# A mixture-of-experts block with adapters: the shared first product by seven half-products over pairs of token groups, staged between the adapter products, and the table entries of all experts fetched together

## The chip, the cores and the metric

One Trainium2 chip, one core of it. The metric is the device time of one execution in microseconds (us), median of three runs. Engines: PE (TensorE, matmuls and weight loads), DVE (VectorE), ACT (ScalarE), POOL (GpSimd) and SP (SyncE, which here only issues transfers). Each engine works through its own instructions in order.

## What is computed

The input is x, 8 batches of 256 tokens, hidden size 1024, in fp32. Every batch has an adapter, chosen by a number in 3 to 7.

```
y      = einsum('bsi,boi->bso', x, weight[adapter_ids])
shared = (silu(g) * u) @ shared_w_down.T,   [g, u] = y @ shared_w_gate_up.T      (1024 -> 2 x 1024 -> 1024)
probs  = softmax(y @ gate_w.T);  the top 2 of 16 experts, their weights made to sum to 1
expert e: (silu(g) * u) @ w_down[e].T,      [g, u] = y @ w_gate_up[e].T          (1024 -> 2 x 256 -> 1024)
out    = x + shared + sum over a token's two experts of weight * expert(y)
```

## The kernel before

**Precision.** A product of fp32 values is made of three matmuls (`mm3`, L73): each operand is split into a high part (a copy rounded to fp32r, on ACT, L59) and a low part (the difference, on DVE, L60); high x high, high x low and low x high are summed in PSUM. `load_w` (L64) brings a weight tile of 128 x 1024 over SP's queue into one of four staging buffers (`st`) and splits it into one of seven buffers of `whl` (`hl`); so PE can have up to seven split tiles ahead of it.

**Tiling.** The 2048 tokens are four groups of 512, each of four blocks of 128 (16 blocks in all).
- `cond(b)` (L145) makes y for the 256 tokens of a batch: 96 matmuls of 512 columns; ACT copies PSUM to `yrow` and puts it in DRAM as `y_d`.
- `group_yt(g)` (L469) reads a group's y back, on POOL's queue (`yr`, L474), transposes it on DVE (L139) and splits it into `yt`.
- `route(g)` (L171): gate logits (16 matmuls of 512 columns, L175), softmax and top 2 on DVE (L194 to L225), each token's rank in its expert by small matmuls (L227 to L237), and eight scatters on POOL (L268), which put the token numbers into a table by expert, `tab_d`. The scatters write one table and go one after the other. The place in the table of a rank below 256 is interleaved (L254 to L260, 264), so that 32 rows with eight entries each can be read as runs.
- `shared_up(g)` (L284): 16 weight tiles of `sgu` x 24 matmuls of 512 columns (`sps`), SwiGLU on ACT and DVE (L278), the result split into `ht`. Four groups: 1536 matmuls.
- `shared_down(g)` (L307): 192 matmuls (`dps`) of a group; DVE adds them to `acc` (L325), which goes to DRAM.
- `experts` (L457): the experts in the order of their token counts, with a fixed capacity of 256 to 304 tokens each. `expert_rows` (L431) reads the entries of one expert (`ib`), POOL makes them places (`ix`, L428) and gathers rows of y in pieces of 256 columns (`yg`, L351); DVE transposes; 96 matmuls of 256 to 304 columns a half (`eps`); the down product (`ops`) goes to `os_d`.
- `combine` (L328): two gathers of rows of `os_d` for a block (L331, POOL), each multiplied and added on DVE (L337).

**Order.** The calls at the end of the function (L478 to L576) give the order; a scheduler then sets the order of each engine's instructions within it, from a model of their times. The order is: the first two adapter products, group 0, cond(2), route(0), half of shared_up(0), cond(3), the other half, group 1, cond(4), route(1), half of shared_down(0), and so on to route(3); shared_up(3), entries and rows of experts 0 and 1, shared_down(3); the 16 experts; shared_up(1) with the combine of eight blocks between its tiles, shared_down(1), shared_up(2) with eight more, shared_down(2). The rows of `combine` and the y blocks share four buffers (`yg`).

## Time and profile before

| | before |
|---|---|
| median of three runs | 1067.23 us (1064.14 to 1073.18) |
| profiled execution: span from first to last instruction | 1060.8 us |
| mean granted TensorE clock | 0.992 of full speed |
| PE busy | 1029.5 us (97%), 5181 matmuls |
| DVE, ACT, POOL busy | 657.7, 466.4, 292.1 us |
| moved by DMA | 243.86 MB, 230 GB/s on the mean |

The page of the profile gives for the profiled execution its span alone; no time of that execution around the span is recorded, so the span stands beside the median.

In the profile a group is a line of the kernel with an engine, an operation and a tile shape; "out<-in" are tile names; after the bar come busy time, mean ns of one, and the idle time of the engine before them with what ended it. In the forty slices a digit is the busy share in tenths, PEclk the granted clock in tenths. A row of the table by stretches gives the length, and for PE, PEld, DVE, ACT and POOL the busy us and the count, then PE's granted clock, the share of DMA time and GB/s. A row of waits gives us in total, times, and the longest. A landing time runs from a transfer's issue to its end. A row of the timeline gives start, length, and in brackets the idle time before it.

### The profile page before, as it was taken

What the parts mean: (1) busy time and instruction counts of PE and PEld (TensorE: products, weight loads), DVE (VectorE), ACT (ScalarE), POOL (GpSimd) and SP (SyncE); (2) the same over time, 40 slices, a digit from 0 to 9 for tenths busy, and PEclk for the clock granted to TensorE, in tenths of its full rate; (3) what the DMA queues carried; (4) which work ended last, traced back from release to release, by engine and by line L of the source; (5) the groups of instructions that cost most, each with busy time, mean ns of one, the idle gap of its engine ahead of it and who ended that gap; (6) DMA issues with size and microseconds to landing.
All of it is one profiled execution on the core that took longest, in us unless ns stands there. A gap on an engine that the chain in (4) does not pass through costs nothing.

```text
span 1060.8 us, 14494 instructions
## 1 busy us (share of the span) xinstructions
PE 1029.5 (97%) x5181; PEld 875.8 (83%) x5181; DVE 657.7 (62%) x918; ACT 466.4 (44%) x626; POOL 292.1 (28%) x332
## 2 busy tenths in 40 slices
PE   6989999999899899999999999999999999999997
PEld 5877888888677688889999999989988888888886
DVE  5676543765567745546877878777784768537321
ACT  5564342544344423314667666566473233122200
POOL 1000210001200223644666656545203423002000
PEclk9999999999899999999999999999999999999999
DMA  7986384567677443655788888787979987827201
GB/s 257 345 301 219 105 253 140 204 232 215 223 249 253 135 159 88 220 189 186 237 283 275 291 271 282 249 273 251 340 262 358 408 344 264 318 92 258 80 33 50
DMA packets 82557, 243.86 MB, mean 230 GB/s; under 512 B 14204, under 2 KB 23164, under 8 KB 82476
## 3 DMA queue, kind: packets, MB, share of 16 engines
q1 hardware_dynamic: 56060, 186.46, 52.6%
q0 software_dynamic: 15856, 47.87, 13.0%
q10 hardware_dynamic: 10560, 8.52, 2.4%
q8 instruction: 42, 0.69, 0.2%
q14 instruction: 39, 0.32, 0.1%
HBM read 203.11 MB, written 39.69 MB: 229 GB/s over the span
## 4 chain that ended last, share of the span: by engine, by line
PE 57%; DMA 5%; issue 5%; POOL 3%; DVE 3%; ACT 1%; POOLq 0%; DVEq 0%; ACTq 0%
PE sps L76 8%; PE sps L75 8%; PE sps L74 8%; PE dps L76 4%; PE dps L75 4%; PE dps L74 4%; PE eps L76 4%; PE eps L74 4%; PE eps L75 4%; POOL yg L351 3%; PE ops L76 2%; PE ops L75 1%; DMA y_d<-yrow 1%; PE ops L74 1%; PE ops L419 1%
## 5 line engine op out<-in xcount | busy, mean ns | idle before, releaser
L60 DVE TENSOR_TENSOR hl<-st,hl 128x1024 fp32r<-128x1024 f32 (+1 forms) x274 | 330.1, 1209 | 180.0 <-ACT hl L59 178.9
L59 ACT CAST hl<-st 128x1024 fp32r<-128x1024 f32 (+1 forms) x274 | 283.5, 1043 | 254.8 <-PE sps L76 79.0
L76 PE MATMUL sps<-yt,hl 128*128 128x512 f32 x512 | 199.5, 390 | 0.0
L75 PE MATMUL sps<-yt,hl 128*128 128x512 f32 x512 | 199.4, 389 | 0.0
L74 PE MATMUL sps<-yt,hl 128*128 128x512 f32 x512 | 198.9, 390 | 0.0
L351 POOL DMA_INDIRECT yg<-y_d,ix x128 | 149.9, 1171 | 40.1 <-issue 35.1
L74 PE MATMUL eps<-yte,hl 128*128 128x256 f32 (+6 forms) x512 | 147.6, 289 | 0.1
L76 PE MATMUL eps<-yte,hl 128*128 128x256 f32 (+6 forms) x512 | 147.5, 288 | 0.0
L75 PE MATMUL eps<-yte,hl 128*128 128x256 f32 (+6 forms) x512 | 147.0, 287 | 0.0
L76 PEld LDWEIGHTS sps<-yt,hl 128*128 128x128 f32 x512 | 96.1, 188 | 20.0
L74 PEld LDWEIGHTS sps<-yt,hl 128*128 128x128 f32 x512 | 96.2, 188 | 19.9
L75 PEld LDWEIGHTS sps<-yt,hl 128*128 128x128 f32 x512 | 96.1, 188 | 19.9
L74 PE MATMUL cps<-hl 128*128 128x512 f32 x256 | 100.8, 398 | 7.6 <-ACT hl L59 7.6
L75 PE MATMUL cps<-hl 128*128 128x512 f32 x256 | 102.2, 399 | 3.2 <-DVE hl L60 3.2
L76 PE MATMUL cps<-hl 128*128 128x512 f32 x256 | 101.7, 397 | 0.0
L76 PE MATMUL dps<-hl,ht 128*128 128x512 f32 x256 | 99.8, 390 | 0.0
L75 PE MATMUL dps<-hl,ht 128*128 128x512 f32 x256 | 99.6, 389 | 0.0
L74 PE MATMUL dps<-hl,ht 128*128 128x512 f32 x256 | 99.6, 389 | 0.0
L74 PEld LDWEIGHTS eps<-yte,hl 128*128 128x128 f32 x512 | 96.4, 188 | 1.1 <-DVE s L378 0.5
L75 PEld LDWEIGHTS eps<-yte,hl 128*128 128x128 f32 x512 | 96.5, 188 | 0.7
L76 PEld LDWEIGHTS eps<-yte,hl 128*128 128x128 f32 x512 | 96.3, 188 | 0.0
L474 POOL DMA_DIRECT2D yr<-y_d x24 | 13.4, 559 | 239.9 <-DMA y_d<-yrow 189.7
(153 smaller groups left out, 1307.5 us busy)
## 6 DMA issues: line engine op xcount, KB each, us to landing
st<-sgu SPq DMA_DIRECT2D x64, 512.0 KB, 3.7
st<-wgu SPq DMA_DIRECT2D x64, 512.0 KB, 3.8
st<-wc SPq DMA_DIRECT2D x63, 512.0 KB, 4.7
st<-sd SPq DMA_DIRECT2D x32, 512.0 KB, 3.9
st<-wd SPq DMA_DIRECT2D x32, 512.0 KB, 5.2
os_d<-o SPq DMA_DIRECT2D x32, 512.0 KB, 5.7
yr<-y_d POOLq DMA_DIRECT2D x24, 512.0 KB, 6.3
y_d<-yrow ACTq DMA_DIRECT2D x16, 512.0 KB, 8.9
```

The source lines that it names most:

```text
L59: nc.scalar.copy(hi, src)
L60: nc.vector.tensor_tensor(lo, src, hi.bitcast(F32), op=ALU.subtract)
L74: nc.tensor.matmul(ps, lhs[0], rhs[0], start=first, stop=False)
L75: nc.tensor.matmul(ps, lhs[0], rhs[1], start=False, stop=False)
L76: nc.tensor.matmul(ps, lhs[1], rhs[0], start=False, stop=last)
L351: nc.gpsimd.indirect_dma_start(out=r[:, t * 256 : (t + 1) * 256], out_offset=None, in_=y_d.rearrange("k a p f -> (k a p) f"), in_offset=ba ...
L419: nc.tensor.matmul(ps, a3[:, fi, :], w[fi][:, l, hs], start=(fi == 0 and l == 0), stop=(fi == 1 and l == 1))
L474: nc.gpsimd.dma_start(r, y_d[g * NB + k].rearrange("a (i t) f -> (a i) (t f)", t=4))
```

## The change

**Seven half-products.** For a pair of groups the product y x sgu is written as a 2 x 2 product: y is halved in the hidden dimension (b1., b2.) and in the pair's groups (b.1, b.2), the weights into four quarters (gate and up by the two halves). Seven products of halves, on sums of halves, take the place of eight: 4 x 24 x 7 = 672 matmuls of 512 columns a pair, before 768. They come in stages: a (two products), b (two), c (one) and d (two), four steps u each. Partial results are kept in fp32 in SBUF (`X`, `S`, `G`); stages b and c begin by copying `X` into PSUM on ACT (`seeded`). Sums of the y halves are made on DVE (`sums`). Sums of the weights are made on DVE for the first pair, stored in DRAM (`ss_d`, ACT's queue) and loaded as weights for the second. The operand halves are split into a ring of four buffers.

**Staging.** For the pair of groups 0 and 1 the stages stand between the adapter products cond(3) to cond(7) and the routes; for the pair of groups 2 and 3 they come after the experts, with the combine of the blocks between the steps. Shared_down(0) and (1) now stand between route(3) and the experts, (2) and (3) at the end.

**Routing.** Groups 1 to 3 are routed from blocks of 128 columns (64 matmuls of 128 columns in place of 16 of 512). The inputs are permuted ahead of the launch so that a table place is the rank itself.

**Entries.** The entries of experts 0 and 1 are read after route(3), those of the other 14 together after the rows of expert 1, with one set of `ix` for all.

**Buffers.** `whl` has five buffers, seven among the experts; PSUM is seven banks in a fixed turn; `combine` has two buffers for its rows (`cr`) and two for its sums (`ca`); pools are opened and closed by phase.

```diff
-    whl = ctx.enter_context(tc.tile_pool(name="whl", bufs=7))
-    big = ctx.enter_context(tc.tile_pool(name="big", bufs=2))
-    rows = ctx.enter_context(tc.tile_pool(name="rows", bufs=3))
+    whl = ctx.enter_context(tc.tile_pool(name="whl", bufs=5))
+    ttp = ctx.enter_context(tc.tile_pool(name="ttp", bufs=2))
...
+    banks = [pacc.tile([P, 512], F32, tag=f"acc{k}", name=f"acc{k}") for k in range(7)]
+    turn = [0]
+    def bank():
+        turn[0] += 1
+        return banks[turn[0] % 7]
...
+    def transpose_to(dst, r, nt):
         nc.vector.transpose(
-            tv.rearrange(order, t=nt),
+            dst.rearrange("p b (t i) -> p t b i", t=nt),
             r[:, : nt * 256].rearrange("p (t b j) -> p t b j", t=nt, b=NC),
         )
+    def transposed(r, nt):
+        tt = ttp.tile([P, 1024], F32, tag="tt", name="tt")
+        tv = tt[:, : NC * 32 * nt].rearrange("p (b n) -> p b n", b=NC)
+        transpose_to(tv, r, nt)
+        return tv
...
+    def route(g, parts):
         lp = psm.tile([P, GT], F32, tag="sm", name="lp")
-        for c in range(NC):
-            for l in range(2):
-                nc.tensor.matmul(lp, gpk[:, c * 2 * E : c * 2 * E + P], yt[:, l, c, :], start=(c == 0 and l == 0), stop=(c == NC - 1 and l == 1))
+        n0 = 0
+        for get, n in parts:
+            for c in range(NC):
+                for l in range(2):
+                    nc.tensor.matmul(
+                        lp[:, n0 : n0 + n],
+                        gpk[:, c * 2 * E : c * 2 * E + P],
+                        get(c)[l],
+                        start=(c == 0 and l == 0),
+                        stop=(c == NC - 1 and l == 1),
+                    )
+            n0 += n
...
-            # place of rank 32t + i: 8i + t below MAIN, the rank itself from MAIN on
-            v.tensor_scalar(ov, rank, float(MAIN), None, op0=ALU.is_lt)
-            v.tensor_scalar(tq, rank, -15.5, 1.0 / 32, op0=ALU.add, op1=ALU.mult)
-            v.tensor_copy(sli, tq)
-            v.tensor_copy(tq, sli)
-            v.tensor_scalar(u, rank, 7.0, None, op0=ALU.mult)
-            v.scalar_tensor_tensor(u, tq, -255.0, u, op0=ALU.mult, op1=ALU.add)
-            v.tensor_tensor(u, u, ov, op=ALU.mult)
...
-            v.tensor_tensor(sl, sl, u, op=ALU.add)
...
-    def shared_up(yt, ht, fs=range(SI // P), also=None):
-        for f in fs:
-            pp = []
-            for j in range(2):
-                w = load_w(sgu[j * (SI // P) + f])
-                ps = pacc.tile([P, GT], F32, tag="acc", name="sps")
-                for c in range(NC):
...
+    def y_block(tb, ys):
+        r = ys.tile([P, 1024], F32, tag="yr", name="yr")
+        nc.gpsimd.dma_start(r, y_d[tb].rearrange("a (i t) f -> (a i) (t f)", t=4))
+        return r
...
+    def operand(ring, src):
+        t = []
+        for k in range(2):
+            op = ring.tile([P, 2, 2, 512], FR, tag="op", name="op")
+            split(op[:, 0], op[:, 1], src[:, 2 * k : 2 * k + 2, :])
+            t.append(op)
+        return t
...
+    def blocks_of(srcs):
+        for src in srcs:
+            t = whl.tile([P, 2, NC, P], FR, tag="whl", name="rb")
+            split(t[:, 0], t[:, 1], src)
+            yield (lambda c, t=t: [t[:, l, c, :] for l in range(2)]), P
...
+    class Up:
+        def __init__(self, first, raw, X, S, G, ring, ys, g0):
+            self.first, self.raw, self.X, self.S, self.G, self.ring, self.ys, self.g0 = first, raw, X, S, G, ring, ys, g0
+        def rows(self, n):
+            for k in range(NB):
+                r = y_block((self.g0 + n) * NB + k, self.ys)
+                transpose_to(self.raw[n][:, :, k * P : (k + 1) * P], r, 4)
+        def half(self, k, n):
+            return self.raw[n][:, 4 * k : 4 * k + 4, :]
+        def begin(self):
+            self.b11 = operand(self.ring, self.half(0, 0))
+            self.b21 = operand(self.ring, self.half(1, 0))
+        def sums(self):
+            v = nc.vector.tensor_tensor
+            t2 = self.S
+            for k in range(2):
+                q = slice(2 * k, 2 * k + 2)
+                b11, b12, b21, b22 = (self.half(r, n)[:, q, :] for r, n in ((0, 0), (0, 1), (1, 0), (1, 1)))
+                t = t2[:, q, :]
+                v(b12, b12, b11, op=ALU.subtract)
+                v(t, b22, b12, op=ALU.subtract)
+                v(b21, b21, t, op=ALU.subtract)
+                v(b11, t, b11, op=ALU.subtract)
+            self.t2 = operand(self.ring, t2[:, 0:4, :])
+            self.t3 = operand(self.ring, self.half(0, 0))
+            pair = lambda a: [a[:, 2 * k : 2 * k + 2, :].rearrange("p a n -> p (a n)") for k in range(2)]
+            at = pair(self.half(0, 0))
+            self.spare_b = [at, pair(self.S[:, 4:8, :]), at, at]
+            self.spare_d = [at, pair(self.half(1, 0))] * 2
+        def product(self, ps, w, m, ops, first):
+            for c in range(4):
+                lhs = [w[:, l, (4 * m + c) * P : (4 * m + c + 1) * P] for l in range(2)]
+                rhs = chunk(ops, c)
+                for i, (x, y) in enumerate(((0, 0), (0, 1), (1, 0))):
+                    nc.tensor.matmul(ps, lhs[x], rhs[y], start=(first and c == 0 and i == 0), stop=(c == 3 and i == 2), skip_group_check=True)
...
+        def made(self, i, u, st):
+            hl = whl.tile([P, 2, 1024], FR, tag="whl", name="shl")
+            split(hl[:, 0, :], hl[:, 1, :], st)
+            nc.scalar.dma_start(ss_d[i, u], st)
+            return hl
+        def sums_b(self, u):
+            if not self.first:
+                return load_w(ss_d[1, u]), load_w(ss_d[2, u])
+            v = nc.vector.tensor_tensor
+            a11, a21 = self.spare_b[u]
+            nc.gpsimd.dma_start(a11, sgu[0, 0, u])
+            nc.gpsimd.dma_start(a21, sgu[1, 0, u])
+            a22 = wst.tile([P, 1024], F32, tag="wst", name="a22")
+            nc.sync.dma_start(a22, sgu[1, 1, u])
+            v(a11, a11, a21, op=ALU.subtract)
+            v(a21, a21, a22, op=ALU.add)
+            v(a22, a22, a11, op=ALU.subtract)
+            w = self.made(1, u, a22), self.made(2, u, a11)
+            nc.scalar.dma_start(ss_d[0, u], a21)
+            return w
+        def sums_d(self, u):
+            if not self.first:
+                return load_w(ss_d[0, u]), load_w(ss_d[3, u])
+            s2, a12 = self.spare_d[u]
+            nc.gpsimd.dma_start(s2, ss_d[1, u])
+            nc.gpsimd.dma_start(a12, sgu[0, 1, u])
+            nc.vector.tensor_tensor(a12, a12, s2, op=ALU.subtract)
+            return load_w(ss_d[0, u]), self.made(3, u, a12)
+        def stage_a(self, u):
+            w1, w2 = load_w(sgu[0, 0, u]), load_w(sgu[0, 1, u])
+            ps = [bank() for m in range(2)]
+            for m in range(2):
+                self.product(ps[m], w1, m, self.b11, True)
+                nc.scalar.copy(self.X[:, 2 * u + m, :], ps[m])
+            for m in range(2):
+                self.product(ps[m], w2, m, self.b21, False)
+                nc.scalar.activation(self.G[:, 2 * u + m, :], ps[m], AF.Silu)
+        def seeded(self, u):
+            ps = [bank() for m in range(2)]
+            for m in range(2):
+                nc.scalar.copy(ps[m], self.X[:, 2 * u + m, :])
+            return ps
+        def stage_b(self, u):
+            w1, w2 = self.sums_b(u)
+            ps = self.seeded(u)
+            for m in range(2):
+                self.product(ps[m], w1, m, self.t2, False)
+                nc.scalar.copy(self.S[:, 2 * u + m, :], ps[m])
+            for m in range(2):
+                self.product(ps[m], w2, m, self.t3, False)
+                nc.scalar.copy(self.X[:, 2 * u + m, :], ps[m])
+        def stage_c(self, u):
+            if u == 0:
+                self.t4 = operand(self.ring, self.half(1, 0))
+            w = load_w(sgu[1, 1, u])
+            ps = self.seeded(u)
+            for m in range(2):
+                f = 2 * u + m
+                self.product(ps[m], w, m, self.t4, False)
+                nc.vector.tensor_tensor(self.G[:, f, :], self.G[:, f, :], ps[m], op=ALU.mult)
+        def stage_d(self, u):
+            if u == 0:
+                self.t1 = operand(self.ring, self.half(0, 1))
+                self.b22 = operand(self.ring, self.half(1, 1))
+            w1, w2 = self.sums_d(u)
+            ps = [bank() for m in range(2)]
+            for m in range(2):
+                f = 2 * u + m
+                self.product(ps[m], w1, m, self.t1, True)
+                nc.vector.tensor_tensor(self.X[:, f, :], ps[m], self.X[:, f, :], op=ALU.add)
+            for m in range(2):
+                f = 2 * u + m
+                self.product(ps[m], w2, m, self.b22, False)
+                nc.vector.tensor_tensor(self.S[:, f, :], ps[m], self.S[:, f, :], op=ALU.add)
+                nc.scalar.activation(self.S[:, f, :], self.S[:, f, :], AF.Silu)
+                nc.vector.tensor_tensor(self.S[:, f, :], self.S[:, f, :], self.X[:, f, :], op=ALU.mult)
...
+    def combine(rows, tb, base, dst):
+        ts = slice(tb * P, (tb + 1) * P)
+        a = rows.tile([P, 1024], F32, tag="ca", name="ca", bufs=2)
+        nc.sync.dma_start(a, base[ts, :])
+        for si, cw in ((s1i, c1), (s2i, c2)):
+            r = rows.tile([P, 1024], F32, tag="cr", name="cr", bufs=2)
+            nc.gpsimd.indirect_dma_start(
+                out=r,
+                out_offset=None,
+                in_=os_d[:, :],
+                in_offset=bass.IndirectOffsetOnAxis(ap=si[:, tb : tb + 1], axis=0),
+            )
+            nc.vector.scalar_tensor_tensor(a, r, cw[:, tb : tb + 1], a, op0=ALU.mult, op1=ALU.add)
+        nc.sync.dma_start(dst[ts, :], a)
...
+    def entries(ns):
+        for n in ns:
+            e = expert_id(n)
+            w = -(-CAPS[n] // 32)
+            nc.sync.dma_start(ib[:, n, :w], tab_d[ds(e * SLOTS, 32 * w), :].rearrange("(t i) o -> i (t o)", i=32))
+        segments(ix[:, ns[0] : ns[-1] + 1, :], ib[:, ns[0] : ns[-1] + 1, :])
...
+    up = Up(True, raw, X, S_, G, ring, ys, 0)
+    up.rows(0)
+    cond(2, ys)
+    up.begin()
+    route(0, [(lambda c: chunk(up.b11 if c < 4 else up.b21, c % 4), GT)])
+    cond(3, ys)
+    up.stage_a(0)
+    up.rows(1)
+    up.stage_a(1)
+    route(1, blocks_of([raw[1][:, :, k * P : (k + 1) * P] for k in range(NB)]))
+    up.stage_a(2)
+    up.stage_a(3)
+    cond(4, ys)
+    up.sums()
+    up.stage_b(0)
+    up.stage_b(1)
+    cond(5, ys)
+    up.stage_b(2)
+    up.stage_b(3)
+    cond(6, ys)
+    route(2, blocks_of(transposed(y_block(2 * NB + k, ys), 4) for k in range(NB)))
+    up.stage_c(0)
+    up.stage_c(1)
+    cond(7, ys)
+    up.stage_c(2)
+    up.stage_c(3)
+    for u in range(4):
+        up.stage_d(u)
+    route(3, blocks_of(transposed(y_block(3 * NB + k, ys), 4) for k in range(NB)))
+    close(px, pr)
...
+    entries([0, 1])
+    e0 = expert_rows(pa[1], 0)
+    shared_down(0, G, ring, ys, x, xs_d)
+    yt = expert_yt(pa[1], e0)
+    rs = expert_rows(pa[1], 1)
+    entries(range(2, E))
+    shared_down(1, S_, ring, ys, x, xs_d)
...
+    def some(k):
+        for tb in left[:k]:
+            combine(ys, tb, x if tb >= 2 * NB else xs_d, xs_d if tb >= 2 * NB else out)
+        del left[:k]
+    for u in range(4):
+        up.stage_a(u)
+        some(1)
+    up.sums()
+    for u in range(4):
+        up.stage_b(u)
+        some(1)
+    for u in range(4):
+        up.stage_c(u)
+        some(u % 2)
+    for u in range(4):
+        up.stage_d(u)
+        some(1)
+    close(px)
+    pc = pool("pc", 4)
+    shared_down(2, G, ring, pc[1], xs_d, out, ["acc"] * NB)
+    some(2)
+    shared_down(3, S_, ring, pc[1], xs_d, out, ["acc"] * NB)
```

## The prediction

> **What bounds the kernel now.** I read the busy row and the forty slices first, then the table by stretches, then the timeline of PE around one gap, then what DVE and POOL wait for, the groups, and the landing times.
>
> ```profile
> span 1060.8 us, 14494 instructions
> ...
> PE 1029.5 (97%) x5181; PEld 875.8 (83%) x5181; DVE 657.7 (62%) x918; ACT 466.4 (44%) x626; POOL 292.1 (28%) x332
> ...
> PE   6989999999899899999999999999999999999997
> ...
> PEclk9999999999899999999999999999999999999999
> ```
>
> PE is the bound: 31.3 us of the span are idle, in slices 1 to 3, 11, 14 and 40.
>
> ```profile
> 106.00:160.00 54.00, 54.00 (x244) 44.55 (x243) 26.44 (x51) 21.89 (x26) 10.77 (x9) 1.00 0.59 181
> ...
> 266.00:320.00 54.00, 48.41 (x193) 38.31 (x192) 33.13 (x35) 21.81 (x26) 8.54 (x8) 0.91 0.71 235
> 320.00:373.00 53.00, 47.06 (x205) 37.45 (x204) 37.89 (x108) 20.52 (x23) 9.18 (x9) 0.97 0.61 197
> ```
> ```profile
> 266.33 0.39 PE L74 MATMUL cps<-hl 128*128 128x512 f32 x1
> 269.37 0.79 PE L75 MATMUL cps<-hl 128*128 128x512 f32 x1 [2.65 <-DVE hl L60]
> 269.96 0.63 PE L76 MATMUL cps<-hl 128*128 128x512 f32 x1
> 270.39 0.63 PE L74 MATMUL cps<-hl 128*128 128x512 f32 x1
> ```
>
> The matmuls overlap, so the 390 ns of a group is not their price; the spacing of starts is: 45 of 512 columns between 14.78 and 25.00 us, 0.227 each. After a gap of 2.65 us they start 0.43 apart (269.96, 270.39): the granted clock is half. Four such spells cost 2.45, 2.05, 1.5 and 1.65 us, 7.6 in all. Work at full pace is thus 1060.8 - 31.3 - 7.6 = 1021.9; the start (7.6 until the first weights are split, 0.5, 2.5 of half clock) and the tail (6.7) are 17.3; the stalls between, clock included, 21.6.
>
> ```profile
> DVE tt L139 <- DMA yg<-y_d,ix: 31.3, 5, 14.0
> ...
> DVE sli L256 <- DMA tab_d<-tid,sli: 22.5, 3, 10.2
> ```
> ```profile
> r<-os_d,s1i POOLq DMA_INDIRECT x16, 7.7
> r<-os_d,s2i POOLq DMA_INDIRECT x16, 7.9
> ```
> ```profile
> yr<-y_d POOLq DMA_DIRECT2D x24, 512.0 KB, 6.3
> y_d<-yrow ACTq DMA_DIRECT2D x16, 512.0 KB, 8.9
> ```
>
> DVE is only 62% busy but works in order, and already waits 14.0 us at a stretch for gathers, 10.2 for scatters. PE hardly felt the first: seven split weight tiles lay ahead of it.
>
> **Part by part: what PE loses and gains.** The first product falls from 1536 to 1344 matmuls of 512 columns: 192 x 0.227 = -43.6 us. Routing of groups 1 to 3 trades 48 of 512 columns for 192 of 128: -10.9, and by the nearest row (280 columns start 0.127 apart, 512 0.227, so about 0.43 ns a column plus little) 0.061 each at the least, 0.127 at the most: +11.7 to +24.4; I take 0.075, near the slope, +14.4. Sum: 1021.9 - 43.6 - 10.9 + 14.4 = 981.8; with start and tail unchanged, 999.1 without a stall in between.
>
> **Engines that get more.** DVE: per pair 8 sums of 1024 columns, 14 operand splits, in the first pair 16 weight sums; at 1.23 us (row of L60: 1.21) 46.7 us a first pair, less 16 transposes of 2.00 that become 1.24 and 8 that go. ACT: 32 seeds and 32 drains of PSUM at 0.6, about 38. Neither reaches 80%; as busy time they cost nothing while PE has 980. The transfers grow by the 16 stores of sums on ACT's queue and 24 loads on POOL's, 512 KB each, and by 8 MB of combine's own tiles; the stretch from 800 to 853 us moved 390 GB/s with PE busy 53.0 of 53.0, so 230 on the mean leaves room. ACT issues those stores between its copies; I count nothing for it, since the copies of the next weights are some tiles ahead, and a store that waits for its sum would show as PE waiting on ACT's hl. POOL's loads are item 3. What counts is order, with five weight tiles ahead (27 us at 24 matmuls each) instead of seven (38), two more only among the experts.
>
> **New stalls, by place.** Each is the time until the last thing that PE needs, less PE's work ahead of it.
> 1. First route: the existing 3.4 us stays.
> 2. Stage a, u = 2, after cond(3). Its y is written and read back: 8.9 + 6.3, and issues, 17 us. Behind that wait stand on DVE two transposes, two splits of routing blocks, the eight sums, then the split of a weight: 13 x 1.23 = 16. Ready after 33 us; PE has 96 x 0.227 + 64 x 0.075 = 26.6. Stall 6.
> 3. Stage b: its two loads of weights to be summed are on POOL's queue between the scatters of route(1). A scatter runs 1.26 and the next waits 2.7 more for it (L268: 40.3 us of work, 65.0 of such waits over 24): 4.0 each, three ahead, then landing 4, sums and split 5. 21 us against cond(4)'s 21.8 and the weight that waits on it: 0 to 8, I take 4.
> 4. cond(7): DVE transposes block 12 (17 us after cond(6)) ahead of cond(7)'s splits. PE has half of stage c and the route, about 15: 0 to 10, I take 6.
> 5. Stage d reads stored sums: 1.
> 6. Route(3) to expert 0: about 18.5 us to the ranks, 8 scatters 32, first entries 5, ix 1.2, ten gathers at 1.25 and landing 17.5, three transposes and splits 7, and expert 1's loads beside: 81. Before, it had shared_up(3) and shared_down(3), 576 matmuls or 130 us, as cover; now 384, 87. And DVE has expert 0's transposes ahead of the eviction (L325's work) whose bank PE needs, so a late gather stops PE before expert 0. 0 to 15, I take 8.
> 7. Second pair's y blocks with one buffer, in the last experts: 1.
> 8. Combine within the second Up: 14 of 16 blocks. With two gather buffers a block needs 2 x 1.25 of issue + 7.8 of landing, partly under the block before: 8.8 to 10.3 a block; one step u of stages a, b, d lasts 48 x 0.227 = 10.9, of c 5.5, one block in two. Nearly hidden; L337's own 1.28 twice included in DVE. 0 to 25, I take 6, mostly at c and the first blocks.
> Sum 35.4; spells of half clock after four of these, 1.5 each: 6. Span 999.1 + 35.4 + 6 = 1040.5. The median of the runs lies 6.4 over the profiled span; so 1046.9, said as 1047.
>
> **Two rules weighed.** By "TensorE: Matmul & The Clock Gate", section "What's actually happening", the clock drops after an idle window of about 3.4 us and needs as much activity to return. Here 2.65 us sufficed, with at most 2.05 us lost. By the rule items 4 and 8, in pieces under 3.4, would be free: 3 us less, 1044; by the row every piece of that size pays. I take the row. Against the change speaks "DMA: Bandwidth & Descriptors", "Specifications": at least 512 bytes are wanted for line rate. The entries of the experts become some 4,500 elements of four bytes (they came as runs of 32 bytes for the first 256). The trace has 1 KB in 32 runs landing in 4.9 us and 32 single elements in 3.6; 288 elements may be 5 to 9. Fourteen such transfers lie beside shared_down(1), on SP's queue ahead of its weights: 0 by the rows, up to 14 x 1 us if they hold the queue. I take 0 and keep 10 in the range.
>
> **Rivals.** (A) The forecast: most of the 43.6 comes through, and half is given back in stalls: 1047, own range 1032 to 1060. (B) The order's slack is larger than I think (before, a wait of 10.2 us on scatters cost PE 2.65 and one of 14.0 nothing): stalls as before, 22 with clock; 999.1 + 22 + 6.4 = 1027. (C) The new waits eat the gain: items 2, 3, 4, 6 and 8 at their upper ends, with a halved clock behind each, 60 to 65 with the clock: 1065 to 1070, no change. (D) Slower: combine's gathers. If os_d is read at the 10.3 us that reloads of 512 KB took beside the experts' end, a block costs 2.5 + 10.3 = 12.8, and DVE, which stands on it in order, gives PE its weights 1.9 us late in each of 14 steps, with a halved clock behind each (about 2): 14 x 3.9 = 55 instead of 6, so 1096. It decides from a block time above 12 us. Against it: waits before L337 are only 18.7 us in the trace for 32 gathers, with four buffers. (E) It does not do what it says: matmuls into seeded banks or from the new operand layout run slower than 0.227; 1344 x 0.01 would already be 13. Nothing in the trace speaks for it; all shapes of 512 columns run at one pace.
>
> **How the numbers follow.** A 0.42, B 0.20, C 0.19 (E is in it), D 0.19. The median of the likeliest, 1047, is the prediction. Low 1018: B with stalls of 12. High 1083: C's upper end plus the entries' 10, or D with half of its steps late (1046.9 - 6 + 27 + 10 = 1078, and some clock); what is left out is the rest of D and a little of B. About 1% is what a measurement of this kernel can tell: faster means below 1056.6, slower above 1077.9. Faster: B and nine tenths of A, 0.58; same: the rest of A, most of C, 0.22; slower: D and a little of C, 0.20.
>
> **What would show it.** PE's busy time near 990 to 1000 and x5133: the sum is right. Starts of L372's matmuls 0.227 apart: not E. In the waits of PE: stalls on DVE's splits near cond(3)'s end, at stage b, at cond(7), before expert 0's eps; each is one item. In DVE's waits: cr<-os_d beyond 60 us with PE waiting for hl: D. PE idle under 35 us in all: B. I am wrong if the idle time sits among the experts, whose order I took as unchanged, or if the start or tail grew.

## The result and the profile after

| | before | after |
|---|---|---|
| median | 1067.15 us (1064.14 to 1073.18, 4 runs) | 1082.16 us (1079.90 to 1084.72, 4 runs) |
| profiled execution: span | 1060.8 | 1082.5 (time of that execution 1084.72) |
| mean granted clock | 0.992 | 0.975 |

The change made the kernel slower: ratio 1.0128, 95% interval 1.0078 to 1.0177. The forecast was 1047, range 1018 to 1083; the direction was wrong. Where single runs of one kernel spread by more than 1.5%, the ratios below are taken over its lower runs, the medians over all.

The page of after, its busy row and the slices:

```profile
span 1082.5 us, 14436 instructions
...
PE 1025.5 (95%) x5133; PEld 861.1 (80%) x5133; DVE 697.5 (64%) x910; ACT 514.1 (47%) x698; POOL 293.1 (27%) x296
...
PE   6999998999998999976999999999999899989996
...
PEclk9999999999998999987999999999999999999999
```

The count of matmuls fell as planned, from 5181 to 5133, but busy time stands at 1025.5, not at the 990 to 1000 of the forecast, and 57.0 us of the span are idle instead of 31.3. Slices 18 and 19, where PE was full before, hold the worst of it, with a lowered clock. The waits of PE (us in total, times, longest):

```profile
PE acc L93 <- ACT hl L75: 9.4, 2, 7.5
PE acc L372 <- DVE X L451: 7.9, 4, 3.6
PE acc L93 <- issue: 7.1, 7, 2.5
PE acc L372 <- DVE op L76: 6.7, 2, 4.6
PE acc L94 <- issue: 6.5, 8, 1.6
PE acc L95 <- issue: 3.2, 4, 1.1
```

"issue" is time in which the engine waited for nothing that the profile shows: 16.8 us in 19 pieces. It was not in the forecast at all. The stretches say where (length; busy us and count of PE, PEld, DVE, ACT, POOL; clock, DMA share, GB/s):

```profile
340.00:350.00 10.00, 6.40 (x22) 4.81 (x21) 7.00 (x8) 2.16 (x2) 2.42 (x2) 0.76 0.93 343
450.00:475.00 25.00, 18.49 (x68) 14.12 (x67) 12.70 (x14) 5.65 (x6) 20.27 (x20) 0.86 0.81 272
...
860.00:960.00 100.00, 93.68 (x384) 75.25 (x385) 64.06 (x63) 35.68 (x48) 27.03 (x21) 0.95 0.87 303
```

25 us of full work hold 110 matmuls of 512 columns; 450 to 475 (shared_down(1), with an expert's rows gathered beside it) has 68. PE's timeline there:

```profile
462.18 0.40 PE L95 MATMUL acc<-hl,ht 128*128 128x512 f32 x1
463.00 0.39 PE L93 MATMUL acc<-hl,ht 128*128 128x512 f32 x1 [0.42 <-issue]
464.43 0.39 PE L94 MATMUL acc<-hl,ht 128*128 128x512 f32 x1 [1.04 <-issue]
465.82 0.40 PE L95 MATMUL acc<-hl,ht 128*128 128x512 f32 x1 [1.00 <-issue]
468.68 0.59 PE L93 MATMUL acc<-hl,ht 128*128 128x512 f32 x1 [2.46 <-issue]
470.85 0.59 PE L94 MATMUL acc<-hl,ht 128*128 128x512 f32 x1 [1.58 <-issue]
```

Operands and weights are there, no semaphore is named, and still the starts stand at about multiples of 0.7 us (0.82, 1.43, 1.39, 2.86, 2.17) instead of 0.234 apart. I call this **creep**. It ends with a row of gathers on POOL:

```profile
467.46 0.95 POOL L514 DMA_INDIRECT yg<-y_d,ix  x1 [0.30 <-issue]
468.47 2.41 POOL L590 TENSOR_SCALAR ix<-ib 32x140 int32<-32x140 int32 x4
```

The last gather goes out at 467.46, and PE's last slow start is at 470.85. A second spell, 495.9 to 512.9 in the first experts, looks the same. By the spacing of starts, with 0.2275 us for 512 columns as nominal, PE lost in after (in all 69.2, before 27.9; lost clock is inside each place): start to 20 us 7.7 (before 3.5); 50 to 192 us, stages a to c of the first pair, 8.9; stage d at 340 to 347, 6.4; creep 9.4 and 16.0; the second pair's product, 800 to 980, 19.4.

### The profile page after: what moved, and what is told of

It reads as the page before. It is cut to its first block, busy times and chain, and to the rows that moved or that the text cites. A ratio compares the mean times of both kernels' runs of the same rounds, so it can differ in the third digit from the quotient of the medians.

```text
span 1082.5 us, 14436 instructions
## 1 busy us (share of the span) xinstructions
PE 1025.5 (95%) x5133; PEld 861.1 (80%) x5133; DVE 697.5 (64%) x910; ACT 514.1 (47%) x698; POOL 293.1 (27%) x296
## 2 busy tenths in 40 slices
DMA packets 90543, 260.65 MB, mean 241 GB/s; under 512 B 18092, under 2 KB 27052, under 8 KB 90460
## 4 chain that ended last, share of the span: by engine, by line
PE 63%; DMA 23%; DVE 5%; issue 5%; ACT 2%; POOL 0%; SPq 0%; ACTq 0%; DVEq 0%; POOLq 0%
PE acc L94 17%; PE acc L95 17%; PE acc L93 16%; PE acc L372 10%; DMA cr<-os_d,s2i 4%; DMA tab_d<-tid,sli 4%; DMA y_d<-yrow 3%; DMA cr<-os_d,s1i 2%; PE acc L582 2%; DMA ca<-xs_d 2%; DMA raw<-sgu 1%; DMA st<-wc 1%; PE lp L208 1%; DVE hl L76 1%; DMA yr<-y_d 1%
## 5 line engine op out<-in xcount | busy, mean ns | idle before, releaser
L372 PE MATMUL acc<-op,hl 128*128 128x512 f32 x1056 | 254.5, 401 | 13.0 <-DVE op L76 6.7
L372 PEld LDWEIGHTS acc<-op,hl 128*128 128x128 f32 x1056 | 201.7, 192 | 61.9 <-DVE op L76 7.5
L94 PE MATMUL acc<-yte,hl 128*128 128x256 f32 (+6 forms) x512 | 149.3, 292 | 3.9 <-issue 3.9
L93 PE MATMUL acc<-yte,hl 128*128 128x256 f32 (+6 forms) x512 | 148.5, 290 | 4.3 <-issue 4.2
L95 PE MATMUL acc<-yte,hl 128*128 128x256 f32 (+6 forms) x512 | 149.1, 291 | 2.3 <-issue 2.2
L94 PE MATMUL acc<-hl 128*128 128x512 f32 x256 | 103.1, 403 | 5.2 <-DVE hl L76 5.0
L94 PE MATMUL acc<-hl,ht 128*128 128x512 f32 x256 | 102.3, 400 | 2.6 <-issue 2.6
L93 PE MATMUL acc<-hl,ht 128*128 128x512 f32 x256 | 101.7, 400 | 2.9 <-issue 2.9
L94 PEld LDWEIGHTS acc<-yte,hl 128*128 128x128 f32 x512 | 97.5, 190 | 8.8 <-issue 8.0
L95 PE MATMUL acc<-hl 128*128 128x512 f32 x256 | 102.5, 400 | 0.0
L95 PE MATMUL acc<-hl,ht 128*128 128x512 f32 x256 | 101.5, 399 | 1.0 <-issue 1.0
L93 PE MATMUL acc<-hl 128*128 128x512 f32 x256 | 92.9, 399 | 9.5 <-ACT hl L75 9.4
L95 PEld LDWEIGHTS acc<-yte,hl 128*128 128x128 f32 x512 | 97.5, 190 | 3.2 <-issue 3.2
L93 PEld LDWEIGHTS acc<-yte,hl 128*128 128x128 f32 x512 | 97.6, 191 | 3.0 <-issue 2.3
L505 DVE SCALAR_TENSOR_TENSOR ca<-cr,c,ca 128x1024 f32<-128x1024 f32 x32 | 41.1, 1283 | 59.6 <-DMA cr<-os_d,s2i 25.3
L372 PE MATMUL acc<-op,shl 128*128 128x512 f32 x288 | 71.7, 405 | 3.6 <-DVE X L451 3.6
L372 PEld LDWEIGHTS acc<-op,shl 128*128 128x128 f32 x288 | 55.7, 194 | 17.5 <-ACT shl L75 4.0
L93 PEld LDWEIGHTS acc<-hl 128*128 128x128 f32 x256 | 49.1, 192 | 21.2 <-ACT hl L75 11.0
```

What stands on the lines that cost most here:

```text
L93: nc.tensor.matmul(ps, lhs[0], rhs[0], start=first, stop=False)
L94: nc.tensor.matmul(ps, lhs[0], rhs[1], start=False, stop=False)
L95: nc.tensor.matmul(ps, lhs[1], rhs[0], start=False, stop=last)
L372: nc.tensor.matmul(ps, lhs[x], rhs[y], start=(first and c == 0 and i == 0), stop=(c == 3 and i == 2), skip_group_check=True)
L505: nc.vector.scalar_tensor_tensor(a, r, cw[:, tb : tb + 1], a, op0=ALU.mult, op1=ALU.add)
```

## Experiments

Sixteen kernels were run. "Loss" is PE's loss by spacing as above, in the profiled execution.

**The experts' entries.** The creep lies beside the small transfers of the entries, which the forecast had at nothing. First they were put back to each expert's turn:

```
-    entries(range(2, E))
...
         if n + 2 < E:
+            entries([n + 2])
             rs = expert_rows(pa[1], n + 2)
```

> The changed kernel with the entries of experts 2 to 15 read one expert at a time, two experts ahead, inside the expert loop. In the changed kernel PE creeps from 462 to 471 us and from 496 to 513 us, one weight load or matmul each 0.7 us, waiting for nothing that the profile names: 25 us with the half clock behind it. Theory B (burst: some 4,000 four-byte elements within 13 us stop the delivery of PE's code): both spells go, 1082 - 25 = 1057. Theory G (gathers: the spells begin 17 and 25 us into an unbroken row of gathers on POOL and end with it): the rows are broken by the waits for each expert's entries, so both go too, 1057. Rival L (a backlog of the 512 KB loads that stand at the same place): both stay, 1082.

Measured: 1147.73 us (1143.8 to 1156.9), ratio 1.0808 [1.0748, 1.0868]. The first spell stayed (9.3 us, 457 to 467) and the second went. The experts now lost some 5 us each (69 us from 516 to 800), PE waiting above all for DVE's `s` (27.7 us in nine pieces): the entries stand behind weights on SP's queue and come late, so POOL waits 100.5 us for them (`ib`, eleven times, 12.3 at the longest), and DVE stands 111.7 us for the rows gathered after that, ahead of `s` in its order. All theories missed this. Fetching the entries at once is thus no cost of the change: undoing it costs 66 us with this order of SP.

Next, the same entries as 32 runs of 32 to 40 bytes, which permutes the rows among an expert's slots:

```
-.rearrange("(t i) o -> i (t o)", i=32)
+.rearrange("(i t) o -> i (t o)", i=32)
```

> The changed kernel with each expert's entries read in 32 runs of 32 to 40 bytes instead of 256 to 320 single elements, all experts at once as before; the rows of an expert then come in another order, so its results belong to other tokens. Theory B: the spells of creeping PE go, 1057. Theory G: the row of gathers on POOL is as long as before, both spells stay, 1082 within 3. Theory L: they stay as well.

Measured: 1078.67 (1062.3 to 1088.7, 20 runs), 1.0071 [1.0044, 1.0097]. Both spells stayed (8.5 and 7.6). A burst of four-byte elements doesn't make the creep. The runs spread widely; whether spells come and go from run to run is not shown, since one run of each kernel left a trace.

**The combine.** Its gathers and multiply-adds are left out, the base rows alone are copied, so the experts' results are missing:

```
-            combine(ys, tb, ...)
...
+            nc.sync.dma_start(a, (x if tb >= 2 * NB else xs_d)[ts, :])
+            nc.sync.dma_start((xs_d if tb >= 2 * NB else out)[ts, :], a)
```

> The changed kernel without the gathers and the two multiply-adds of combine: a block's base is loaded and stored only, so the experts' results are left out of the output. PE loses 19 us in the second Up and stages of it (800 to 1000 us). Theory C (DVE stands in order on combine's gathers and gives PE its operands late): 15 to 19 of these go, 1064 to 1067. Rival O (the operand splits and sums of the stage changes themselves are late, whatever combine does): at most 5 go, 1077 or more. The spells at 462 to 513 us stay in both.

Measured: 1064.27 (12 runs, one at 1045.9 and eleven from 1061.7 to 1074.9), 18 below after; the runs scatter by more than that, but each lies below after's lowest. The losses of the second product went from 19.4 to none, the creep stayed at 8.0 and 16. So two separate costs, of 19 and 25 us, stand behind the result. This is how the first works, in DVE's timeline of after around PE's largest stall, the 4.6 us from PE's waits above:

```profile
852.15 1.28 DVE L505 SCALAR_TENSOR_TENSOR ca<-cr,c,ca 128x1024 f32<-128x1024 f32 x1 [2.70 <-DMA ca<-x]
857.65 1.28 DVE L505 SCALAR_TENSOR_TENSOR ca<-cr,c,ca 128x1024 f32<-128x1024 f32 x1 [4.21 <-DMA cr<-os_d,s2i]
858.85 1.22 DVE L76 TENSOR_TENSOR hl<-st,hl 128x1024 fp32r<-128x1024 f32 x1
859.99 2.35 DVE L76 TENSOR_TENSOR op<-S,op 128x1024 fp32r<-128x1024 f32 x2
```
```profile
853.76 2.91 PE L372 MATMUL acc<-op,hl 128*128 128x512 f32 x12
861.26 2.08 PE L372 MATMUL acc<-op,hl 128*128 128x512 f32 x4 [4.59 <-DVE op L76]
```

From 849.4 to 857.6 DVE does 1.28 us of work: it stands 2.70 us for a block's base rows and 4.21 for a gather. The splits behind it come at 858.85 and 859.99, and PE, done at 856.7, waits until 861.26 for them. DVE is only 64% busy; its order is the cost.

So I held each multiply-add behind the last split or product that the step needs, and moved half of the blocks into shared_down(2) and (3) (the lines of stages c and d, which keep one block each at u == 1, are left out here):

```
-            nc.vector.scalar_tensor_tensor(a, r, ...)
+            with tc.issue_after(last_dve[0].ins):
+                nc.vector.scalar_tensor_tensor(a, r, ...)
...
         up.stage_a(u)
-        some(1)
+        some(int(u < 3))
...
         up.stage_b(u)
-        some(1)
+        some(int(u > 0))
...
+    some(4)
     shared_down(2, ...)
-    some(2)
+    some(4)
```

> The changed kernel with combine's multiply-adds held behind DVE's work for the step that they follow, and half of the blocks moved from the second Up into the last two shared_down. Theory C (DVE stands on combine's gathers ahead of splits that PE needs): of the 19 us that PE loses from 800 to 1000 us, 10 to 15 come back, 1067 to 1072. If the order in the first stages alone decides it: less than 6, 1076 or more.

Measured: 1043.59 (1042.1 to 1047.5), 0.982 [0.978, 0.9861]: 38.6 below after. The second product:

```profile
860.00:960.00 100.00, 100.00 (x437) 81.75 (x436) 60.95 (x66) 39.83 (x48) 7.11 (x6) 1.00 0.57 190
```

Its loss went from 19.4 to 0.9; theory had 10 to 15 of it. Which of the two parts did it, the holding or the moving, was not separated. The other half of the gain is luck: both spells of creep were gone too, 300 us ahead of the first changed instruction, and a plain wait of 3.0 us for DVE's eviction (L490's work) stood in their place. A kernel without creep is thus no proof that its edit removed it.

**The start.** ACT's store of a weight sum waits for DVE's hoisted sum, and the next weight's copy stands behind it (ACT's timeline of after):

```profile
14.28 1.04 ACT L75 CAST hl<-st 128x1024 fp32r<-128x1024 f32 x1 [1.19 <-DMA st<-wc]
17.75 0.34 ACTq L378 DMA_DIRECT2D ss_d<-S  x1
18.13 1.99 ACT L75 CAST hl<-st 128x1024 fp32r<-128x1024 f32 x2 [2.81 <-DVE S L390]
```

The sum for t2 goes where stage b's own results come later, so that it can't be made early:

```
-            t2 = self.S
+            t2 = self.S[:, 4:8, :]
```

> The changed kernel with the first half of the y sums kept in the other half of S, so that the weight sums of step 1 of stage b, which use that place, can't run before those sums. In the changed kernel they run at 16.5 us, and ACT's store of them at 17.75 stands ahead of the weights of the first adapter product. Theory H (this hoist costs the start its 4 us): PE's loss before 20 us falls from 7.7 to about 3.5, and the sums cost 2 or so in stage b: 1078 to 1081. Rival (the start is late for its loads alone): 1082 or more.

Measured: 1078.1 (1065.3 to 1090.7), 1.0116 [1.0087, 1.0144]; loss at the start 3.45, as before the change. The creep was there, 19.9 and 5.

**What makes the creep.** One theory was the length of the row of gathers, with four `yg` buffers that let 16 or more go out without a pause (part of one line):

```
-tag="yg", bufs=4, name="yg"
+tag="yg", bufs=2, name="yg"
```

> The changed kernel with two buffers instead of four for the gathered rows of y, so that POOL must wait for DVE's transposes after eight to ten gathers; the entries are still fetched all at once. The spells of creeping PE have ended, in all five traces so far, within 3 us of the end of an unbroken row of 17 or more gathers. Theory G (PE's code does not arrive while such a row runs): both spells go, 25 us less, 1057, unless the gathers now come too late for the experts. Theory L (backlog of large loads at that place): spells stay, 1082.

Measured: 1061.46 (1058.3 to 1069.0), 0.9971 [0.9949, 0.9993]. No creep, though the profiled run was the slowest (a wait of 3.5 for DVE's eviction instead). But rows of 14, 23 and 17 gathers were still there, with the DMA share at 0.93 or more from 445 to 460: the time is right and the reason not confirmed. From the other side, the kernel before was given a long row (16 more gathers ahead of an expert's own, 26 in all from 433.4 to 468.6), and in another kernel a backlog of transfers (32 unused loads of 512 KB in shared_up(3)):

```
+        for i in range(4 if n == 1 else 0):
+            gather_rows(ix, 4 * (i % 2), 4)
```
```
+            for k in range(4):
+                with tc.issue_after(last_load[0].ins):
+                    nc.sync.dma_start(busy[0][k], x[k * P : (k + 1) * P, :])
```

> The kernel before with sixteen more gathers of rows of y ahead of expert 1's own (read again and not used), which makes one row of 26 gathers where it had 10; no four-byte elements are added. Theory G: PE creeps for 5 to 15 us about 17 us into the row and stops doing so at its end, with waits put down to no releaser: 1075 to 1085. Rivals B and L: no creep, at most the delay of expert 1's rows, 1064 to 1070.

> The kernel before with 32 loads of 512 KB from x into tiles that are not used, four ahead of each step of shared_up(3), on SP's queue. Theory L: within the 90 us of shared_up(3) PE reaches three ends of a block of code; where the DMA engines are at nine tenths or more for 10 us ahead of it, PE creeps with waits put down to issue, 5 us or more in all. Rival: PE waits only for its weights (hl), which come later, and no wait is put down to issue.

Measured: 1063.19, 1.000 [0.998, 1.0019], and 1065.39, 1.0014 [0.9995, 1.0034]. Neither creeps. The stretch of the row, and that of the backlog:

```profile
450.00:460.00 10.00, 10.00 (x46) 8.29 (x45) 1.30 (x3) 2.62 (x3) 7.57 (x8) 1.00 0.54 157
```
```profile
376.00:396.00 20.00, 20.00 (x90) 16.39 (x89) 17.74 (x64) 6.22 (x8) 2.75 (x3) 1.00 1.03 409
```

A row with the queues half empty (0.54) costs nothing; full queues (1.03) without a row cost nothing, though they were tried some 70 us earlier. In the first spell of after both come together; in the second, larger one the queues are not full (0.75, 0.73):

```profile
450.00:460.00 10.00, 10.00 (x44) 8.07 (x43) 3.58 (x3) 1.05 (x1) 7.82 (x8) 1.00 0.86 257
460.00:470.00 10.00, 4.34 (x15) 2.47 (x14) 4.25 (x5) 3.55 (x4) 7.98 (x10) 0.91 1.00 362
...
490.00:500.00 10.00, 7.32 (x45) 6.42 (x43) 4.24 (x5) 2.33 (x2) 7.86 (x8) 0.94 0.75 219
500.00:510.00 10.00, 4.51 (x12) 2.96 (x11) 0.00 (x0) 0.00 (x0) 7.56 (x9) 0.50 0.73 257
```

And both together are not enough. In the late combine PE until 983 us, and POOL to the end, carry out the same instructions in the same order as in after; the row is there, the queues are full, and PE runs free:

```profile
450.00:460.00 10.00, 10.00 (x44) 8.05 (x43) 4.82 (x4) 1.77 (x2) 7.59 (x8) 1.00 1.01 352
```

Taking load away there, by replacing the loads of `acc` in shared_down(1) by zeros (x is left out of that group's output):

```
-                nc.sync.dma_start(acc[k], base[ts[k], :])
+                if g == 1:
+                    nc.vector.memset(acc[k], 0.0)
+                else:
+                    nc.sync.dma_start(acc[k], base[ts[k], :])
```

> The changed kernel with the four loads of x for shared_down(1), 512 KB each, replaced by setting these tiles to zero, so x is left out of the second group's output. They stand in one burst of eight 512 KB loads beside the gathers; the DMA engines are over nine tenths busy for 16 us, and the first spell of creeping PE lies in it. Theory L (PE's next block of code comes due, each 128 matmuls, while such a backlog is there): the first spell goes or halves, 5 to 9 us less, 1073 to 1077, the second stays or moves. If neither the backlog nor the moment matters: 1082.

Measured: 1061.99 (1048.9 to 1073.2, 20 runs), 0.9948 [0.9926, 0.997], both spells gone. In the place of the second the queues are now fuller than in after (0.91 from 490 to 500, 0.99 from 500 to 510), so the load taken away does not explain that one.

A third candidate is PE's own program. The profile has a queue of kind "instruction" (q8 on the page, 42 packets, 0.69 MB, so 16 KB each); a packet comes about every 29 us of PE's work, per 128 matmuls with their 128 weight loads. In after they lie at 404.5, 434.3, 473.5 and 514.1, the last two just after a spell. They are late in time but not by the count of matmuls (130 and 129 after the one before), so their lateness follows from PE's own delay. To test whether the place in these blocks matters, 80 more transposes were put into route(0), which shift the ends of these blocks against the work; then 128, one whole block, which put them back:

```
-            nc.tensor.transpose(lt[:, k, :], ...)
+            for i in range(21 if g == 0 else 1):
+                nc.tensor.transpose(lt[:, k, :], ...)
```

> The changed kernel with eighty more small transposes on PE in route(0) (they write again what is there), about 5 us of work, which moves the end of each later block of PE's code 80 matmuls, some 18 us, ahead; the transfers keep their places. Theory L: code comes due near 447 and 484 us plus the 5 of the shift instead of 463 and 496, mostly outside the backlog, and the spells shrink from 25 us to under 12: 1082 + 5 - 13 or less, 1074 or less. If the code's place does not matter: 1087.

> The changed kernel with 128 more small transposes on PE in route(0) instead of eighty: some 8 us of work, but the ends of PE's blocks of code fall on the same work again as in the changed kernel. If the place of the code's ends is what made the spells go with eighty: the spells come back, 1082 + 8 = 1090, and at the least 1075. If the delay of all later work by a few us was enough: no spells, 1062 to 1067.

Measured: with 80 more, 1062.42 (1050.8 to 1070.7, 20 runs), 0.9973 [0.995, 0.9995]; with 128 more, 1093.69 (1089.6 to 1096.4), 1.0249 [1.0212, 1.0285]. PE did more work in both. First the stretches with 80, then with 128:

```profile
450.00:475.00 25.00, 22.35 (x96) 17.68 (x95) 13.32 (x15) 5.66 (x6) 19.87 (x21) 1.00 0.93 303
500.00:525.00 25.00, 25.00 (x161) 23.31 (x160) 21.67 (x32) 16.08 (x27) 20.12 (x17) 1.00 0.93 310
```
```profile
475.00:485.00 10.00, 5.59 (x18) 4.00 (x17) 6.25 (x9) 4.09 (x5) 8.12 (x10) 0.83 0.96 344
505.00:531.00 26.00, 11.74 (x42) 9.41 (x41) 6.81 (x9) 7.07 (x9) 14.01 (x14) 0.61 0.63 195
```

With 80 the queues are as full (0.93) and the row on POOL is as dense (19.87 of 25), and PE runs free; what PE idles there is a plain wait for DVE. That the spells go says little, since seven other variants of after lost them too. With 128 they are back, 6.1 and 20.4 us, which speaks for the place. Last, all of it was put into the kernel **before**: the row of extra gathers and twelve DRAM copies of 512 KB, issued at 427 to 442, where a packet of PE's code had come at 449 with the row alone:

```
+        for i in range(4 if n == 1 else 0):
+            gather_rows(ix, 4 * (i % 2), 4)
...
+                if g == 3 and h == 1 and q == 0:
+                    with tc.issue_after(last_load[0].ins):
+                        for i in range(12):
+                            nc.sync.dma_start(junk[i][:, :H], x[i * P : (i + 1) * P, :])
```

> The kernel before with both at once, the row of 26 gathers ahead of expert 1 and twelve copies of 512 KB from x to DRAM that nothing reads, on SP's queue after the first weights of the second half of shared_down(3). Each of the two alone (the row; loads for 90 us) left PE's code on time. Theory M (code is late where a long row of gathers and a backlog of large transfers meet and an end of a block falls into it): PE creeps for 5 us or more near 450 to 460 us with waits put down to issue. If it takes neither together: only waits for weights, which the copies delay.

Measured: 1087.11 (two runs), 1.0195 [1.0158, 1.0232]. Its timeline of PE and the stretches around it:

```profile
455.68 0.39 PE L76 MATMUL dps<-hl,ht 128*128 128x512 f32 x1
455.90 0.39 PE L77 MATMUL dps<-hl,ht 128*128 128x512 f32 x1
457.73 0.40 PE L78 MATMUL dps<-hl,ht 128*128 128x512 f32 x1 [1.44 <-issue]
458.45 0.49 PE L76 MATMUL dps<-hl,ht 128*128 128x512 f32 x1 [0.32 <-issue]
461.27 0.59 PE L77 MATMUL dps<-hl,ht 128*128 128x512 f32 x1 [2.33 <-issue]
464.82 0.59 PE L78 MATMUL dps<-hl,ht 128*128 128x512 f32 x1 [2.96 <-issue]
```
```profile
440.00:450.00 10.00, 10.00 (x45) 8.26 (x45) 2.24 (x3) 1.22 (x2) 7.84 (x8) 1.00 1.03 371
450.00:460.00 10.00, 7.18 (x30) 5.39 (x29) 0.26 (x1) 1.33 (x2) 7.57 (x8) 1.00 0.95 332
460.00:471.00 11.00, 2.88 (x5) 1.20 (x5) 6.79 (x7) 3.27 (x4) 8.54 (x7) 0.52 0.44 137
```

The packet comes at 465.1, eleven matmuls later than with the row alone (matmul 1874 instead of 1863), and the kernel that did not creep now does for 16.8 us, by steps of about that kind (starts 1.83, 0.72, 2.82, 3.55 apart). It goes on to about 471 although the queues are half empty by then (0.44): it ends with the row, whose last gather starts at 469.70. So with the row in place, the copies bring the creep. The copies without the row were not run at this place.

Thirteen spells lie in the traces of seven kernels: after, five of its variants, and this one. All end 1.9 to 4.4 us after the last gather of an unbroken row of 10 to 27. Twelve begin within the last 25 matmuls ahead of a packet, one (the second with entries in runs) 74 ahead of it. A row of gathers is thus shown for every spell, and a place near the end of a block of code for nearly every one. Neither is enough, nor are full queues needed. In after and the late combine the runs of each lie close together (1079.9 to 1084.7 and 1042.1 to 1047.5), so there the built program decides it and not the single run. What sets it off stays open.

By the Trainium skill, "Runtime: NRT & Kernel Launch", section "Instruction fetch mechanics", PE's code comes in blocks of 16 KB, 256 instructions, through a queue of the sequencer's own, into a store of 2048 instructions, and a crossing is mostly hidden. The block size agrees with the packets here. PE lost 9.4 and 16.0 us close to two packets; that the crossing is the cause is not shown, and no run here shows how much code lies ahead of PE.

**The pace.** The starts in shared_down(1) are 0.234 apart in after, 0.227 in the kernel before, as means over their undisturbed rows. By the addresses in the built programs, the new operand tiles of after begin 224 bytes (first pair and `at`) or 192 bytes (second pair) past a multiple of 256; those of before begin 128 past, but the experts' `at` 160. 64 and 96 bytes of unused SBUF were put ahead of them:

```
+    padl.tile([P, 16], F32, tag="padl", name="padl")
...
+    padr[1].tile([P, 24], F32, tag="padr", name="padr")
```

> The changed kernel with 64 and 96 bytes of unused space in SBUF, so that the operand tiles of the two Ups and of shared_down start at a multiple of 128 bytes as they do in the kernel before. In the changed kernel they start 32, 64 or 96 bytes past one, and the starts of these 2112 matmuls lie 0.2290 to 0.2342 us apart against 0.2268 before. Theory A (the tile's place in SBUF sets this pace): all at 0.2268, 11 us less, 1071 if the spells of creeping PE stay as they are. Rival (the layout of the operand tile, two chunks instead of eight, sets it): no change of pace, 1082.

Measured: 1056.57 (1049.9 to 1063.3), 0.9934 [0.9904, 0.9963]. The first pair's shared_down, now 128 past, went from 0.2345 to 0.2271; the second's, now at a multiple of 256, stayed (0.2334, 0.2333); the experts' down product went from 0.2326 to 0.2279. There the tile is the stationary operand. In the halves' product, where it is the moving one, the first pair went from 0.233 to 0.227 and the second from 0.229 to 0.233. So the start of the operand tile does set the pace, by 3%, and part of what the pads gained in the first pair was lost again in the second. This kernel has no creep either, though PE and the other engines carry out after's instructions in after's order, so its time doesn't price the pace.

**Put together.** First the late combine, the order of t2 and two `yg` buffers; then without the last; then with the pads.

> The changed kernel with three of these edits together: the y sums in the other half of S (start), two buffers for gathered rows, combine held back and half of it late. If the causes are separate, their sums add: 1082 - 4 - 25 - 12 = 1041. If theory G falls, 1066.

> The changed kernel with combine held back and half of it late, and the y sums in the other half of S, gathered rows with four buffers. From 1043.6 with the first edit, less 4 for the start: 1040 if no spell of creeping PE falls into it; 1048 if one does.

> The version that holds combine back and moves half of it late, with the y sums in the other half of S (1040.6), and the same 64 and 96 bytes of unused space. Theory A: 11 less, 1030, PE busy about 1000. Rival: 1040.

Measured: 1048.33 (1043.0 to 1053.2), 0.9869 [0.9826, 0.9913]; **1040.61** (1038.0 to 1044.8), 0.9779 [0.9733, 0.9826]; 1040.88 (1039.2 to 1043.9), 0.9779 [0.9744, 0.9813]. Two buffers, which help alone, cost 8 here. The pads gave nothing more: PE's loss by spacing rose from 25.2 to 35.3. The middle one beats both kernels; its page (span 1036.7 us):

```profile
PE 1005.4 (97%) x5133; PEld 850.3 (82%) x5133; DVE 698.6 (67%) x910; ACT 514.2 (50%) x698; POOL 291.2 (28%) x296
...
PE   6999999999999999989999999999999999999996
```

The change's work saving was real: with creep, combine and start out of the way, 2.2% comes through. The creep went by luck; no edit of this kernel was aimed at it.

## Why the prediction was wrong

Two steps failed most. Item 8 called combine "nearly hidden" and took 6 us; DVE, in order behind combine's transfers, cost PE 19.4. Item 6 took 8 us and assumed that an idle PE always has a releaser; two spells without one cost 25.4, and what sets them off is open. A slower pace, put at nothing, added about 9. Items 1 to 4 and the half clock, 16.5 too dear, hid part of the miss.

Term by term, in us of the span. The right column is the loss in after's trace; lost clock is in each place, not apart.

| term | forecast | measured |
|---|---|---|
| full-pace work | 981.8 | 988.5 |
| slower pace of 512 columns (rival E) | 0 | about 9 (remainder) |
| start and tail | 17.3 | 24.1 |
| items 1 to 4, stages a to c, first pair | 19.4 | 8.9 |
| item 5, stage d | 1 | 6.4 |
| item 6, to expert 0 | 8 | 25.4 (creep) |
| item 7, experts | 1 | 1.1 |
| item 8, combine | 6 | 19.4 |
| half clock, apart | 6 | 0 |
| sum | 1040.5 | 1082.5 |

- **Work.** The count was right. The 192 small matmuls of the routes start 0.110 apart (48 steps in 5.31 us, twice), not 0.075: 21.1 instead of 14.4, within the bounds given. By the Trainium skill, "TensorE: Matmul & The Clock Gate", section "Back-to-back issue gap", pairs of weight load and matmul at 128 columns take about 81 ns; by that figure my estimate would have been 15.6. Neither the slope between 280 and 512 columns nor the rule holds at this width.
- **Pace.** E was put into C as a thing for which nothing in the trace speaks. "All shapes of 512 columns run at one pace" was too quick: `ops` ran at 0.2331 in the kernel before. Of the remainder of 9 (12 when the trace of before is taken as the base), 5.4 is seen directly: 768 matmuls of shared_down x 0.007. The rest is L372, whose rows show 0.229 to 0.233.
- **Start and tail**, "unchanged": wrong by 4.2 at the start, shown by the order of t2, and by 2.0 in the tail, which I did not follow. ACT's stores were put at nothing because "the copies of the next weights are some tiles ahead"; at the start none are. The sign named for it, PE waiting on ACT's `hl`, is there (1.97 us at 15.37).
- **Items 1 to 4.** Item 3 was right, 4.5 against 4, and by its mechanism: DVE stands 2.45 and 3.14 us for two loads of `sgu` that POOL issued late, and PE 2.97 for the split behind. The others were too dear: item 1 1.7 against 3.4, item 2 1.8 against 6, item 4 next to nothing against 6.
- **Item 5.** "Reads stored sums: 1" left out that the first pair still makes one of its sums in stage d, from a load of POOL's behind scatters and y reads: DVE's L403 waited 3.00 us for it, and PE 3.60 for the L451 behind.
- **Item 6.** Its mechanism, an eviction behind expert 0's transposes, is there: 2.7 to 4.7 us where the creep is gone (late combine, two buffers, 80 transposes, pads), within the 8. The 25.4 are creep, in which PE waits for nothing that the profile names. 16.0 of them lie among the first experts, which the text named as a sign of being wrong.
- **Item 8.** The mechanism was named, DVE in order behind combine's transfers, and so was the block time: the blocks' last multiply-adds start at 837.1, 847.0 and 857.6, about 10 us apart, the forecast said 8.8 to 10.3 in a step of 10.9. What failed is the conclusion "nearly hidden". A block that fits on the mean still has DVE standing in it: from 800 to 980 us, 48.8 us for gathers and 10.8 for base rows, which were in no block's time. 19.4 of these reached PE: within the bounds of 0 to 25, but three times the 6 taken. D's mechanism was this one, at a third of its 55.
- **Clock.** The row weighed against the rule held: after the wait of 2.97 us that ended at 184.45 the starts stood 0.43 apart (185.19, 185.61, 186.04), under the 3.4 us of the rule. As a term of its own it was counted on top of losses too large already.
- **Small elements.** Taking the entries at nothing against the rule of 512 bytes held as well as the runs can tell: no wait of PE names them, and runs of 32 to 40 bytes left both spells.
- **Median over span.** I added 6.4; the profiled execution of after took 1084.72 for a span of 1082.5, so 2.2. The 6.4 was the scatter of runs.
- **Transfers.** The "24 loads on POOL's" queue are 16, and combine's tiles brought no 8 MB: the kernel moved 260.65 MB, 16.8 more than before, 8.4 each on ACT's and POOL's queues. No term of the sum rests on this.

Of the rivals C's total (1065 to 1070) came nearest, with some of its reasons: item 8 was near its upper end and E, which C holds, did come, but items 2 to 4 stayed low and the largest cost, the creep, is in no rival. Without the creep alone (1062, as with 80 transposes) the change would have been within 1% of before.

**Open.** What sets the creep off: whether it is the fetch of PE's code at all, what a row of gathers would hold up there, and why kernels whose edit did not touch the place (late combine, two buffers, pads) lost it. Small shifts in time would do it, or other addresses of tiles in memory; neither was tested by itself.

## What to carry over

Ask of every work that is put "between" steps of a bound engine at which instruction of an in-order engine it waits, not whether it fits on the mean; hold it behind what the bound engine needs next. When PE idles with "issue" as the only reason, look at what the DMA queues and POOL's gathers do there, and change something harmless (a tile's address, the place of a few instructions) to see whether the stall stays, before you blame the edit. An experiment whose time comes out right may have lost a stall elsewhere: look at the place, not only at the time.

## What the hardware showed unexpectedly

- PE can lose time with no wait that the profile names: matmuls and weight loads each start one per some 0.7 us or slower, and the spell ends 1.9 to 4.4 us after the last of a row of indirect gathers on POOL (thirteen spells of seven kernels). It cost 25.4 us in after and 16.8 provoked in the kernel before. What sets it off is open.
- Matmuls of 512 columns start 0.2268 to 0.2279 us apart where the operand tile begins 128 bytes past a multiple of 256, and 0.229 to 0.2345 where it begins at 0, 160, 192 or 224.
- Matmuls of 128 columns, each with its weight load, start 0.110 us apart.
- Full DMA queues alone don't slow PE: at a share of 1.03 and 409 GB/s it was busy 20.00 of 20.00 us.
